# Layer 0 of a four-layer network: denominators of 256 queries per column strip, the turning matrix built first, keys on two queues, permuting copies further behind

## The chip, the cores and the metric

The kernel runs on one core of a Trainium2 chip. The metric is device microseconds of one execution of the whole program, all four layers. The core has five engines that run side by side, each in the order of its own instructions: TensorE (PE, with its weight loads as PEld), VectorE (DVE), ScalarE (ACT), GpSimd (POOL) and SyncE (SP), which here only issues DMAs. SyncE, ScalarE and GpSimd can each issue DMAs from a queue of their own; the 16 DMA engines behind the queues are shared.

## The reference

Only layer 0 is touched. It is attention over a 64x64 image with a learned bias for the relative row and the relative column, four heads of 32 channels, two images, all in f32:

```
x = x + conv_ref(group_norm(x))              # x: [2, 64, 64, 128]
q, k, v = split(group_norm(x) @ w_qkv)       # 4 heads of 32, L = 4096 positions
rw[q, m] = q . pos_emb_w[m],  rh[q, m] = q . pos_emb_h[m]   # m: relative column, row
scores = q k^T / sqrt(32) + shifted(rw) + shifted(rh)
out = softmax(scores) @ v
```

The two biases are products of q with the table of embeddings, shifted by one position per row so that a relative index becomes an absolute one (`rel_to_abs`).

## The kernel before

**Tiling.** Layer 0 goes through four units, a unit being one image b and one pair p of heads. A unit has eight query blocks (qb) of 512 queries, and each of these four key blocks (xb) of 1024 keys. For one key block the loop in `layer0` makes eight score tiles of 128 keys by 512 queries by two heads (matmuls at L806), whose exponentials ScalarE writes (L814); VectorE adds every tile into one accumulator `l0acc` (L817, L819), and 32 matmuls with v (L837) add to `l0o`. The accumulator, summed over its 128 partitions, is later the denominator.

**Bias by matmul.** The bias is not added: it is part of the score product. The keys' tile `ka` has, for each head, 32 rows of keys and 32 rows of one-hot patterns (made once on GpSimd by 16 instructions at L330), and the moving tile `l0mv` has 32 rows of q and 32 rows of bias: 16 for the row (`hd`, L681) and 16 for the column (`wd`, L676; for the very first block, four DMAs from `l0rw` in SBUF, L671). `fill` loads one `l0mv` per key block, two buffers in turn; for xb 2 and 3 it only loads `hd` anew. `prefill(at + 2)` at the end of each key block issues the load for two blocks later.

**Making the biases.** `biases` is a generator that yields 17 pieces for one unit. For the column bias, piece k (0 to 7): GpSimd turns q of one group g of 512 (`turned_q`, tile `l0tq`, L596), TensorE multiplies it with the turned embeddings (`l0pw`, L567), ScalarE or VectorE copies the result to SBUF (`l0ew`, L578 and L576), two DMAs store it to DRAM (`l0sw`, L581), two DMAs read it back with a skew (`l0tw`, L623), and GpSimd permutes that into `l0rw` (L605). The whole `l0rw` is stored as `wd` by four DMAs (L629). For the row bias (k from 8 on): `l0ph` (L567), `l0eh`, `l0sh`, and a skewed DRAM to DRAM copy to `hd` (L635).

**Prologue.** Before the loop the code goes once through the group norm of image 0 (`tokens`, norms at L474), `l0_constants` (a reversed identity called flip, made on GpSimd at L283 and L284, and matmuls at L296 that turn the embeddings with it), `project_k` (matmuls L509, copies L517 to `l0kst`, 16 DMAs to `ka`, L530), `project_q` (L541, copies to `l0xT`, four stores to `qd` in DRAM, L557), 11 of the 17 bias pieces of unit 0, and `project_v` (L488). The slope stores of even g go on ScalarE's queue here, all other DMAs on SyncE's. Then `prefill(0)` and `prefill(1)`.

**Side work.** What the later units need (the rest of the biases, the group norm and projections of image 1) is a list of generators per unit, `later`. `piece()` takes one yield of the list; the loop calls it once per key block, between scores and o matmuls, and once more after the o matmuls of xb 3.

**The end of a query block** is spread over the key blocks of the next one: `end_numerators` and `end_totals` at xb 0 (copy of `l0o`, L734; eight matmul instructions with a matrix of ones, `l0zb`, L741, that give the totals for all 512 queries on all four strips of 32 rows; a copy with a sum for a check, L749), `end_scale` at xb 1 (reciprocal on VectorE, 128x512, L752), `end_mult` at xb 2 (one multiply on GpSimd, L755), `end_fold` at xb 3 (matmuls L760 that add the two halves and turn the result, a second checked sum on ScalarE, L767, and the addition to x, L771). The strips 0 and 1 of `l0o` hold one half of the keys for heads 0 and 1, strips 2 and 3 the other half, so that a total is needed on both halves of the rows.

**What sets the order.** Layer 0 is under a manual schedule: each engine runs its instructions in the order in which the code writes them. So what stands ahead in the text on GpSimd's or SyncE's queue is waited for. The completion of DMAs on SyncE's and ScalarE's queues is counted on a set of semaphores shared by both, so an issue also waits until an earlier transfer that used the same semaphore has landed.

Of the kernel before, what the change touches and what calls it, by code (L numbers as in the profile page):

```python
# [8 lines left out]
F32 = mybir.dt.float32  # L9
# [29 lines left out]
class Net:  # L39
# [236 lines left out]
            )  # L276
        return raw

    def l0_constants(self, wp, ap, ps, raw):

        nc = self.nc
        flip = ap.tile([P, 512], F32, tag="os", name="l0flip")[:, :P]
        nc.gpsimd.memset(flip, 0.0)  # L283
        nc.gpsimd.affine_select(  # L284
            out=flip,
            in_=flip,
            compare_op=ALU.not_equal,
            fill=1.0,
            base=2 - 2 * S,
            pattern=[[1, P]],  # L290
            channel_multiplier=1,
        )
        pos = wp.tile([P, 2, P], F32, tag="pos", name="l0pos")
        for i in range(2):
            pt = ps.tile([P, 2, 512], F32, tag="pair", name=f"l0pe{i}")[:, 0, :]
            nc.tensor.matmul(  # L296
                pt[:, :P],
                lhsT=raw[:, i].rearrange("p h d -> p (h d)"),
                rhs=flip,
                start=True,  # L300
                stop=True,
            )
            nc.scalar.copy(pos[:, i, :], pt[:, :P])
        return pos
# [42 lines left out]
    def layer0(self):  # L347
# [7 lines left out]
        with ExitStack() as st:  # L355
# [18 lines left out]
            kd = dp.tile([2 * HD, L], F32, tag="kd", name="l0kd")  # L374

            mvs = [wp.tile([P, NX, 512], F32, tag=f"mv{i}", name=f"l0mv{i}") for i in range(2)]
            kas = self.l0_onehot(wp, ap, 2)

            def scratch(n):
# [38 lines left out]
            def tokens(ps, b):  # L418
# [40 lines left out]
                v = self.small.tile([P, 1], F32, tag="gv", name=f"gv{b}")  # L459
                nc.vector.scalar_tensor_tensor(v, d, d, mv[:, 1:2], ALU.mult, ALU.add)  # L460
                yield
                pv = bank(ps, f"gpv{b}")
                nc.tensor.matmul(pv[:, 0, 0:1], lhsT=self.gmat, rhs=v, start=True, stop=True)
                gr = self.small.tile([P, 1], F32, tag="gr", name=f"gr{b}")
# [39 lines left out]
            def project_k(ps, b):  # L504

                for x in range(NX):
                    pk = bank(ps, f"l0pk{b}_{x}")
                    for s in range(2):
                        nc.tensor.matmul(  # L509
                            pk[:, s, :].rearrange("p (a k) -> p a k", k=P),  # L510
                            lhsT=w[:, C : 2 * C],
                            rhs=halves(norm[b, x])[:, s],
                            start=True,
                            stop=True,
                        )
                    kst = staging(f"l0kst{b}_{x}").rearrange("p n q -> p (n q)")
                    nc.scalar.activation(  # L517
                        halves(kst),
                        pk.rearrange("p s (a k) -> p s a k", k=P),
                        AF.Copy,  # L520
                        scale=root,
                    )
                    cols = slice(x * TB * S, (x + 1) * TB * S)
                    for p in range(pairs):
                        if (b, p) == (1, 1):
                            nc.sync.dma_start(out=kd[:, cols], in_=kst[2 * HD :])
                            continue
                        for h in range(2):
                            at = (2 * p + h) * HD
                            nc.sync.dma_start(  # L530
                                out=kas[p][64 * h : 64 * h + HD, cols], in_=kst[at : at + HD]
                            )
                    yield

            def project_q(ps, b):

                xT = qTs[b]
                for x in range(NX):
# [18 lines left out]
                    nc.sync.dma_start(out=qd[b][:, cols], in_=xT[:, cols])  # L557
                    yield

            def slope(ps, u, n, g, tq):  # L560
# [25 lines left out]
            def biases(hold, u):  # L586
# [6 lines left out]
                def turned_q(g):  # L593
# [4 lines left out]
                        qTs[b].rearrange("p (x y) -> p y x", y=S)[:, 8 * g : 8 * g + 8, :],  # L598
                    )

                turned_q(0)
                for k in range(2 * 8 + 1):
                    if 2 <= k < 10:
                        g = k - 2
                        nc.gpsimd.tensor_copy(  # L605
                            rw.rearrange("p (x y) -> p y x", y=S)[:, 8 * g : 8 * g + 8, :],
                            tws.pop(g),
                        )
                    if k < 7:
                        turned_q(k + 1)  # L610
                    if 1 <= k < 9:
                        g = k - 1
                        if loop[0]:
                            tws[g] = ap.tile(
                                [P, 8, S], F32, tag="tw", name=f"l0tw{b}_{p}_{g}", bufs=1
                            )
                        elif g % 2 == 0:
                            tw2 = ap.tile(
                                [P, 2, 8, S], F32, tag="acc", name=f"l0tw{b}_{p}_{g}"
                            )  # L620
                            tws[g], tws[g + 1] = tw2[:, 0], tw2[:, 1]
                        for h in range(2):
                            nc.sync.dma_start(  # L623
                                out=tws[g][S * h : S * h + S],
                                in_=skewed(slopes[h, "w"][u], 8 * g, S, 8),
                            )
                    if k == 9:
                        for c in range(0, L, L // 4):
                            nc.sync.dma_start(  # L629
                                out=wd[u][:, c : c + L // 4], in_=rw[:, c : c + L // 4]  # L630
                            )
                    if k >= 9:
                        g = k - 9
                        for h in range(2):
# [22 lines left out]
            def fill(mv, u, qb, xb):  # L657
                b, p = u
                qs = slice(qb * 512, (qb + 1) * 512)
                for h in range(2):  # L660
                    at = (2 * p + h) * HD
                    if xb < 2:
                        near = u == units[0] and qb == 0
                        q = (qTs if near else qd)[b]
                        nc.sync.dma_start(
                            out=mv[64 * h : 64 * h + HD], in_=wide(q[at : at + HD, qs], HD)
                        )
                        if near:
                            for s in range(NX):
                                lo = 64 * h + TB * s  # L670
                                nc.sync.dma_start(  # L671
                                    out=mv[64 * h + 48 : 64 * h + 64, s],
                                    in_=rws[u][lo : lo + TB, qs],
                                )
                        else:
                            nc.sync.dma_start(  # L676
                                out=mv[64 * h + 48 : 64 * h + 64],
                                in_=wd[u][:, qs].rearrange("(h s r) q -> h r s q", h=2, r=TB)[h],
                            )
                    lo = S * h + S - TB * (xb + 1)  # L680
                    nc.sync.dma_start(  # L681
                        out=mv[64 * h + 32 : 64 * h + 48], in_=wide(hd[u][lo : lo + TB, qs], TB)
                    )

            first = [None]
            with tc.tile_pool(name="l0sp", bufs=4, space=PSUM) as ps:
                hold = [ps]
                for _ in tokens(ps, 0):
                    pass
                pos = self.l0_constants(wp, ap, ps, raw)  # L690
                for _ in project_k(ps, 0):
                    pass
                for _ in project_q(ps, 0):
                    pass
                first[0] = biases(hold, units[0])
                for _ in range(11):
                    next(first[0])
                for _ in project_v(ps, 0):
                    pass
# [34 lines left out]
                nc.scalar.copy(e.os, e.o)  # L734

            def end_totals(e):
                zb = ps.tile([P, 512], F32, tag="misc", name=f"l0zb{e.t}")
                for s in range(2):
                    for h in range(2):
                        at = 64 * s + HD * h  # L740
                        nc.tensor.matmul(  # L741
                            zb[at : at + HD, :],
                            lhsT=ones,
                            rhs=e.acc[:, h, :],
                            start=True,
                            stop=True,
                        )
                e.r = ap.tile([P, 512], F32, tag="zs", name=f"l0zs{e.t}", bufs=1)
                nc.scalar.activation(e.r, zb, AF.Copy, accum_out=sums[:, 0, e.n : e.n + 1])  # L749

            def end_scale(e):
                nc.vector.reciprocal(e.r, e.r)  # L752

            def end_mult(e):
                nc.gpsimd.tensor_tensor(e.os, e.os, e.r, ALU.mult)  # L755

            def end_fold(e):
                po = ps.tile([P, 4, 2 * HD], F32, tag="misc", name=f"l0po{e.t}")
                for i in range(4):
# [4 lines left out]
                        start=True,  # L764
                        stop=True,
                    )
                nc.scalar.activation(e.r, e.r, AF.Copy, accum_out=sums[:, 1, e.n : e.n + 1])  # L767
                b, p = e.u
                n0 = b * NC + 4 * e.qb
                xs = self.x[:, n0 : n0 + 4, p * 64 : p * 64 + 64]  # L770
# [8 lines left out]

            prefill(0)  # L780
            prefill(1)
            cur, prev = None, None
            for at, (i, qb, xb) in enumerate(order):
                u = units[i]
# [37 lines left out]
                if prev:  # L822
# [2 lines left out]
                    elif xb == 1:  # L825
                        end_scale(prev)
                    elif xb == 2:
                        end_mult(prev)
                    else:
                        end_fold(prev)  # L830
                piece()
# [12 lines left out]
                if xb == 3:  # L844
                    piece()
                prefill(at + 2)
            for part in (end_numerators, end_totals, end_scale, end_mult, end_fold):
                part(cur)
            while side:
                piece()  # L850
# [1289 lines left out]
```

## Time and profile before

| | us |
|---|---|
| four runs | 4851.39, 4856.27, 4859.64, 4865.56 |
| median | 4857.95 |
| profiled execution | 4860.4 |
| its span, first to last instruction | 4857.5 |
| layer 0, prologue (to the first full score block) | 0 to 120.8 |
| layer 0, loop and tail | 120.8 to 1671.9 |
| layers 1 to 3 | to 4857.5 |
| reciprocal L752, x32 | 3.34 to 3.35 each |
| multiply L755, x32 | 1.26 to 2.07 each |
| totals L741, eight instructions per block | 0.98 to 0.99 |

Over the span TensorE is busy 89%, VectorE 63%, ScalarE 49% and GpSimd 18%. These shares mix stages: in the prologue TensorE mostly waits (28.25 of 63 us between 54 and 117), and in the loop it is nearly always at work. So the prologue is read from the chain of waits and from the queue's own timeline, and the loop from windows between two reciprocals, one per query block. "SPq" is SyncE's issuing of a DMA, whose length is the time to issue; the landing stands apart, as "DMA".

### The profile page before, as it was taken

To read this page: it belongs to the slowest core of one execution; us is meant where nothing else is said; L and a number is where in the kernel's file an instruction comes from. 1 tells how busy PE (TensorE), PEld (TensorE's weight loads), DVE (VectorE), ACT (ScalarE), POOL (GpSimd) and SP (SyncE) were. 2 spreads that over 40 slices of the span, in tenths; PEclk is the share of its full clock that TensorE was granted. 3 is DMA by queue.
4 is the path that set the end of the run, shared out by engine and by line. 5 is a ranking of instruction groups with operands and counts; after the bars stand their busy time and mean duration, and the time that the engine had idled before them with its cause. 6 is when DMAs were issued, how large, how long until landed. Compare 5 with 4: busy or idle time off the path is not lost.

```text
span 4857.5 us, 67788 instructions
## 1 busy us (share of the span) xinstructions
PE 4326.8 (89%) x27079; PEld 1849.8 (38%) x27079; DVE 3048.0 (63%) x4776; ACT 2379.9 (49%) x2850; POOL 858.5 (18%) x561
## 2 busy tenths in 40 slices
PE   4999999999999755689999999949999999999765
PEld 2233333323333244322332333329974444444422
DVE  2898888989999888456666555550043333333577
ACT  1776677767766433257776888810022222222200
POOL 4110020210000121135554555500020000000000
PEclk6999999999999877789999999955589999999889
DMA  5452344453333100000000000023300000000000
GB/s 150 103 125 51 70 100 113 90 120 64 59 54 64 32 1 1 25 1 1 1 1 1 1 1 1 1 72 104 104 2 0 1 0 0 0 0 0 6 13 23
DMA packets 200790, 189.11 MB, mean 39 GB/s; under 512 B 83626, under 2 KB 137738, under 8 KB 200266
## 3 DMA queue, kind: packets, MB, share of 16 engines
q1 hardware_dynamic: 177546, 165.71, 15.5%
q10 hardware_dynamic: 22912, 18.89, 1.3%
q8 instruction: 218, 3.57, 0.3%
q14 instruction: 114, 0.93, 0.1%
HBM read 143.13 MB, written 45.09 MB: 39 GB/s over the span
## 4 chain that ended last, share of the span: by engine, by line
PE 68%; DVE 21%; ACT 4%; issue 3%; DMA 2%; POOL 1%; SPq 1%; DVEq 0%; ACTq 0%; POOLq 0%
PE l0sc L806 11%; DVE l0acc L819 10%; PE scl L1904 9%; PE oTl L1921 9%; PE l0o L837 5%; PE l2sc L1533 5%; PE l2pos L1434 4%; PE l2av L1585 4%; PE f3ex L2078 3%; PE f2po L1782 2%; PE f2ph L1756 2%; ACT l2es L1571 2%; DVE x L2086 1%; PE l2pu L1418 1%; DVE l2es L1557 1%
## 5 line engine op out<-in xcount | busy, mean ns | idle before, releaser
L819 DVE TENSOR_TENSOR l0acc<-l0acc,l0es 128x1024 f32<-128x1024 f32 x960 | 1226.0, 1277 | 125.5 <-ACT l0es L814 30.1
L814 ACT ACTIVATE l0es<-l0sc 128x1024 f32<-128x1024 f32 x1024 | 953.6, 1051 | 362.3 <-PE l0sc L806 342.0
L806 PE MATMUL l0sc<-l0mv,ka 64*64 64x512 f32 x8192 | 921.8, 597 | 18.5 <-issue 13.7
L1929 DVE TENSOR_TENSOR accl<-accl,esl 128x1024 f32<-128x1024 f32 x240 | 294.1, 1225 | 540.8 <-ACT esl L1915 482.8
L1560 POOL TENSOR_TENSOR l2es<-l2es 128x1024 f32<-128x1024 f32 (+3 forms) x288 | 505.6, 1756 | 603.8 <-DVE l2es L1557 533.3
L806 PEld LDWEIGHTS l0sc<-l0mv,ka 64*64 64x64 f32 x8192 | 295.0, 132 | 636.5 <-issue 296.6
L1571 ACT ACTIVATE l2es<-l2es 128x1024 f32<-128x1024 f32 (+3 forms) x576 | 533.3, 976 | 6.9 <-POOL l2es L1564 6.7
L1915 ACT ACTIVATE esl<-scl 128x1024 f32<-128x1024 f32 x240 | 245.8, 1024 | 550.4 <-PE scl L1904 550.4
L1557 DVE TENSOR_SCALAR l2es<-l2sc 128x1024 f32<-128x1024 f32 (+3 forms) x272 | 306.5, 1127 | 296.9 <-PE l2sc L1533 294.2
L1904 PE MATMUL scl<-l3qT,l3kT 128*128 128x512 f32 x1024 | 485.0, 596 | 1.8 <-DVE bok_l L254 1.8
L837 PE MATMUL l0o<-l0es,l0v 128*32 128x512 f32 x4096 | 465.6, 595 | 0.0
L1921 PE MATMUL oTl<-esl,l3v 128*128 128x512 f32 x960 | 448.5, 592 | 0.0
L1547 ACT ACTIVATE l2es<-l2sc 128x1024 f32<-128x1024 f32 (+3 forms) x288 | 273.7, 950 | 260.9 <-PE l2sc L1533 257.9
L1533 PE MATMUL l2sc<-l2q,l2kT 32*128 32x512 f32 (+3 forms) x2304 | 340.2, 624 | 10.1 <-DVE l2es L1557 5.9
L1585 PE MATMUL l2av<-l2es,l2v 128*32 128x512 f32 (+3 forms) x2304 | 321.6, 579 | 8.6 <-ACT l2es L1571 8.5
L1434 PE MATMUL l2pos<-l2v,toe 128*32 128x512 f32 (+3 forms) x2304 | 299.9, 581 | 1.4 <-ACT l2v L1379 1.4
L755 POOL TENSOR_TENSOR l0os<-l0os,l0zs 128x512 f32<-128x512 f32 x32 | 63.2, 1975 | 1300.3 <-DVE l0zs L752 1011.6
L1904 PEld LDWEIGHTS scl<-l3qT,l3kT 128*128 128x128 f32 x1024 | 193.1, 191 | 233.8 <-issue 219.2
L1921 PEld LDWEIGHTS oTl<-esl,l3v 128*128 128x128 f32 x960 | 182.4, 190 | 229.6 <-issue 225.8
L837 PEld LDWEIGHTS l0o<-l0es,l0v 128*32 128x32 f32 x4096 | 121.7, 109 | 311.3 <-issue 309.4
L1533 PEld LDWEIGHTS l2sc<-l2q,l2kT 32*128 32x128 f32 x2304 | 100.7, 189 | 255.3 <-ACT l2es L1571 91.5
L2086 DVE SCALAR_TENSOR_TENSOR x<-f3ex,f3wt,x 128x128 f32<-128x128 f32 x512 | 160.2, 347 | 28.5 <-PE f3ex L2078 20.0
(457 smaller groups left out, 4191.8 us busy)
## 6 DMA issues: line engine op xcount, KB each, us to landing
l0mv<-l0hd SPq DMA_DIRECT2D x256, 128.0 KB
l0mv<-l0qd SPq DMA_DIRECT2D x124, 256.0 KB
l0mv<-l0wd SPq DMA_DIRECT2D x124, 128.0 KB
l0sh<-l0eh SPq DMA_DIRECT2D x60, 144.0 KB
l0tw<-l0sw SPq DMA_DIRECT2D x64, 128.0 KB
l0wd<-l0rw SPq DMA_DIRECT2D x16, 512.0 KB
l0hd<-l0sh SPq DMA_DIRECT2D x64, 128.0 KB
f2w<-in_L_ffn_weight_dram ACTq DMA_DIRECT2D x32, 256.0 KB
```

The costliest lines, as they stand in the source:

```text
L806: nc.tensor.matmul(sc[64 * c : 64 * c + 64, h, :], lhsT=ka[rows, k0 : k0 + 64], rhs=mv[rows, NX - 1 - yb, :], start=True, stop=True,)
L814: nc.scalar.activation(es[yb, s], sc, AF.Exp)
L819: nc.vector.tensor_tensor(cur.acc, cur.acc, es[yb, s], ALU.add)
L837: nc.tensor.matmul(cur.o[lo : lo + HD, :], lhsT=v[:, 2 * (xb * NX + yb) + s, HD * h : HD * (h + 1)], rhs=es[yb, s][:, h, :], start=(xb == ...
L1434: nc.tensor.matmul(pos[c : c + 32, j0:, :], lhsT=toe[:, d * P + c : d * P + c + 32], rhs=v[:, n0 + j0 - d : n0 + 4 - d, :], start=(d == n0 ...
L1533: nc.tensor.matmul(sc[:, h2, off:], lhsT=kT[hs, cols], rhs=q[hs, off:], start=True, stop=True,)
L1557: nc.vector.tensor_scalar(es[:, :, lo:], sc[:, :, lo:], root, None, ALU.mult)
L1560: nc.gpsimd.tensor_tensor(part, part, part, ALU.mult)
L1571: nc.scalar.activation(e[:, :, off:], e[:, :, off:], AF.Silu)
L1585: nc.tensor.matmul(avs[i][hs, off:], lhsT=vs[b][:, k, hs], rhs=es[h // 2][:, h % 2, off:], start=(k == 0), stop=last,)
L1904: nc.tensor.matmul(sc[:, i, :], lhsT=kT[:, k * P : (k + 1) * P], rhs=qs, start=True, stop=True,)
L1921: nc.tensor.matmul(oT, lhsT=v[:, k, :], rhs=es[:, i, :], start=(k == 0), stop=(k == NC - 1),)
```

## The change

- `l0_flip` is split from `l0_constants` and called ahead of the one-hots.
- In the prologue the eight key DMAs of pair 1 are issued by GpSimd rather than SyncE.
- In the prologue the four stores of q to `qd` are taken out of `project_q` and written after `prefill(1)`.
- In the prologue the permuting copies of group g run in piece g + 4 rather than g + 2, and those left at k = 9; so GpSimd's order is tq 0 to 5, copy 0, tq 6, copy 1, tq 7, copies 2 to 7. 10 pieces run before the loop rather than 11.
- The first two fills read the column bias from `wd` in DRAM with one DMA per head rather than four from `l0rw`, 12 DMAs in all rather than 24, and the six of head 1 are issued by ScalarE.
- `tokens` yields once more between the two matmuls of the group statistics (L452 and L463).
- The totals are made for 256 queries per strip pair (half the columns), and so are the checked copy and the reciprocal. At xb 2 ScalarE copies each half across to the other rows (two copies of 64x256) and makes the second checked sum (before: at xb 3), and GpSimd multiplies in four instructions of 64x256.

```diff
@@ layer0
+            flip = self.l0_flip(ap)
             kas = self.l0_onehot(wp, ap, 2)
...
@@ tokens
                 yield
+                yield
                 pv = bank(ps, f"gpv{b}")
...
@@ project_k
-                            nc.sync.dma_start(
+                            queue = nc.gpsimd if p and not loop[0] else nc.sync
+                            queue.dma_start(
                                 out=kas[p][64 * h : 64 * h + HD, cols], in_=kst[at : at + HD]
...
@@ project_q
-                    nc.sync.dma_start(out=qd[b][:, cols], in_=xT[:, cols])
+                    if loop[0]:
+                        nc.sync.dma_start(out=qd[b][:, cols], in_=xT[:, cols])
...
@@ biases
+                    if loop[0] and 2 <= k < 10:
+                        permuted(k - 2)
                     if k < 7:
                         turned_q(k + 1)
+                    if not loop[0] and 4 <= k < 9:
+                        permuted(k - 4)
                     if 1 <= k < 9:
+                        shifted(k - 1)
                     if k == 9:
+                        for g in sorted(tws):
+                            permuted(g)
+                        stored()
...
@@ fill
+                    near = u == units[0] and qb == 0
+                    queue = nc.scalar if near and h and xb < 2 else nc.sync
...
-                        if near:
-                            for s in range(NX):
-                                lo = 64 * h + TB * s
-                                nc.sync.dma_start(
-                                    out=mv[64 * h + 48 : 64 * h + 64, s],
-                                    in_=rws[u][lo : lo + TB, qs],
-                                )
...
@@ prologue
-                for _ in range(11):
+                for _ in range(10):
                     next(first[0])
...
@@ end_totals
-                            rhs=e.acc[:, h, :],
+                            rhs=e.acc[:, h, 256 * s : 256 * s + 256],
...
@@ end_scale, end_cross in place of end_mult
+                nc.vector.reciprocal(e.r[:, 0, :], e.r[:, 0, :])
...
-                nc.gpsimd.tensor_tensor(e.os, e.os, e.r, ALU.mult)
+                for s in range(2):
+                    there, here = slice(64 - 64 * s, 128 - 64 * s), slice(64 * s, 64 * s + 64)
+                    nc.scalar.copy(e.r[there, 1, :], e.r[here, 0, :])
+                nc.scalar.activation(
+                    e.r[:, 0, :], e.r[:, 0, :], AF.Copy, accum_out=sums[:, 1, e.n : e.n + 1]
+                )
+                for s in range(2):
+                    rows = slice(64 * s, 64 * s + 64)
+                    for i in range(2):
+                        part = e.os[rows, 256 * i : 256 * i + 256]
+                        nc.gpsimd.tensor_tensor(part, part, e.r[rows, (s + i) % 2, :], ALU.mult)
...
@@ end_fold
-                nc.scalar.activation(e.r, e.r, AF.Copy, accum_out=sums[:, 1, e.n : e.n + 1])
...
@@ after the first fills
             prefill(0)
             prefill(1)
+            for x in range(NX):
+                cols = slice(2 * x * 512, 2 * (x + 1) * 512)
+                nc.sync.dma_start(out=qd[0][:, cols], in_=qTs[0][:, cols])
```

In `biases` the helpers `permuted`, `shifted` and `stored` hold the code that stood in the loop over k before (L605, L623 and L629).

More of the change, by code (lines that the diff above doesn't have):

```diff
@@ L277, in l0_raw, with l0_flip @@
         return raw
-    def l0_constants(self, wp, ap, ps, raw):
+    def l0_flip(self, ap):
         nc = self.nc
@@ L292, in l0_constants @@
         )
+        return flip
+    def l0_constants(self, wp, ps, raw, flip):
+        nc = self.nc
         pos = wp.tile([P, 2, P], F32, tag="pos", name="l0pos")
@@ L599, in turned_q, with permuted, shifted @@
                     )
+                def permuted(g):
+                    nc.gpsimd.tensor_copy(
+                        rw.rearrange("p (x y) -> p y x", y=S)[:, 8 * g : 8 * g + 8, :],
+                        tws.pop(g),
+                    )
+                def shifted(g):
+                    if loop[0]:
+                        tws[g] = ap.tile([P, 8, S], F32, tag="tw", name=f"l0tw{b}_{p}_{g}", bufs=1)
+                    elif g % 2 == 0:
+                        two = ap.tile([P, 2, 8, S], F32, tag="acc", name=f"l0tw{b}_{p}_{g}")
+                        tws[g], tws[g + 1] = two[:, 0], two[:, 1]
+                    for h in range(2):
+                        nc.sync.dma_start(
+                            out=tws[g][S * h : S * h + S],
+                            in_=skewed(slopes[h, "w"][u], 8 * g, S, 8),
+                        )
@@ L601, in biases, with stored @@
+                def stored():
+                    for c in range(0, L, L // 4):
+                        nc.sync.dma_start(
+                            out=wd[u][:, c : c + L // 4], in_=rw[:, c : c + L // 4]
+                        )
                 turned_q(0)
                 for k in range(2 * 8 + 1):
[L603 to L607, printed above, removed]
-                        )
+                    if loop[0] and 2 <= k < 10:
+                        permuted(k - 2)
@@ L609, in biases @@
                     if k < 7:
                         turned_q(k + 1)
+                    if not loop[0] and 4 <= k < 9:
+                        permuted(k - 4)
                     if 1 <= k < 9:
[L612 to L626, printed above, removed]
+                        shifted(k - 1)
                     if k == 9:
[L628 to L631, printed above, removed]
+                        for g in sorted(tws):
+                            permuted(g)
@@ L661, in fill @@
                     at = (2 * p + h) * HD
+                    near = u == units[0] and qb == 0
+                    queue = nc.scalar if near and h and xb < 2 else nc.sync
                     if xb < 2:
-                        near = u == units[0] and qb == 0
                         q = (qTs if near else qd)[b]
-                        nc.sync.dma_start(
+                        queue.dma_start(
                             out=mv[64 * h : 64 * h + HD], in_=wide(q[at : at + HD, qs], HD)
                         )
-                        if near:
-                            for s in range(NX):
-                                lo = 64 * h + TB * s
-                                nc.sync.dma_start(
-                                    out=mv[64 * h + 48 : 64 * h + 64, s],
-                                    in_=rws[u][lo : lo + TB, qs],
[L674 to L679, printed above, removed]
+                        queue.dma_start(
+                            out=mv[64 * h + 48 : 64 * h + 64],
+                            in_=wd[u][:, qs].rearrange("(h s r) q -> h r s q", h=2, r=TB)[h],
+                        )
                     lo = S * h + S - TB * (xb + 1)
-                    nc.sync.dma_start(
+                    queue.dma_start(
                         out=mv[64 * h + 32 : 64 * h + 48], in_=wide(hd[u][lo : lo + TB, qs], TB)
@@ L689, in layer0 @@
                     pass
-                pos = self.l0_constants(wp, ap, ps, raw)
+                pos = self.l0_constants(wp, ps, raw, flip)
                 for _ in project_k(ps, 0):
@@ L736, in end_totals @@
             def end_totals(e):
-                zb = ps.tile([P, 512], F32, tag="misc", name=f"l0zb{e.t}")
+                zb = ps.tile([P, 512], F32, tag="misc", name=f"l0zb{e.t}")[:, :256]
                 for s in range(2):
@@ L747, in end_totals, with end_cross @@
                         )
-                e.r = ap.tile([P, 512], F32, tag="zs", name=f"l0zs{e.t}", bufs=1)
-                nc.scalar.activation(e.r, zb, AF.Copy, accum_out=sums[:, 0, e.n : e.n + 1])
+                e.r = ap.tile([P, 2, 256], F32, tag="zs", name=f"l0zs{e.t}", bufs=1)
+                nc.scalar.activation(
+                    e.r[:, 0, :], zb, AF.Copy, accum_out=sums[:, 0, e.n : e.n + 1]
+                )
             def end_scale(e):
-                nc.vector.reciprocal(e.r, e.r)
-            def end_mult(e):
-                nc.gpsimd.tensor_tensor(e.os, e.os, e.r, ALU.mult)
+                nc.vector.reciprocal(e.r[:, 0, :], e.r[:, 0, :])
+            def end_cross(e):
+                for s in range(2):
+                    there, here = slice(64 - 64 * s, 128 - 64 * s), slice(64 * s, 64 * s + 64)
+                    nc.scalar.copy(e.r[there, 1, :], e.r[here, 0, :])
+                nc.scalar.activation(
+                    e.r[:, 0, :], e.r[:, 0, :], AF.Copy, accum_out=sums[:, 1, e.n : e.n + 1]
+                )
+                for s in range(2):
[3 more added lines that the diff above has]
+                        nc.gpsimd.tensor_tensor(part, part, e.r[rows, (s + i) % 2, :], ALU.mult)
             def end_fold(e):
@@ L827, in layer0 @@
                     elif xb == 2:
-                        end_mult(prev)
+                        end_cross(prev)
                     else:
@@ L846, in layer0 @@
                 prefill(at + 2)
-            for part in (end_numerators, end_totals, end_scale, end_mult, end_fold):
+            for part in (end_numerators, end_totals, end_scale, end_cross, end_fold):
                 part(cur)
```

## The prediction

> **What bounds it now.** Two parts of layer 0 are touched: the prologue up to 120.8 us and the loop to 1661.8; the rest (to 4857.5) is not. I read the chain of waits for the first 260 us first. Columns: start, length, what (us).
> ```profile
> 24.96 9.28 POOL ka L330 x4
> ...
> 34.30 0.20 POOL l0flip L283
> ...
> 34.57 0.29 POOL l0flip L284
> 34.87 18.26 issue
> ...
> 53.17 1.03 POOL l0tq L596
> ...
> 59.86 4.82 DMA l0sw<-l0ew
> ...
> 65.42 4.10 DMA l0tw<-l0sw
> ...
> 117.60 3.11 DMA l0mv<-l0hd
> 120.70 0.09 issue
> 120.79 9.16 PE l0sc L806 x58
> ```
> GpSimd's one-hots hold the turning matrix until 34.9, and TensorE's projections stand behind it; then a chain of small transfers runs to 120.8. Next, SyncE's timeline and its waits:
> ```profile
> 40.64 18.34 SPq L530 DMA_DIRECT2D ka<-l0kst  x16
> 59.41 4.11 SPq L557 DMA_DIRECT2D l0qd<-l0xT  x4
> 64.69 1.52 SPq L623 DMA_DIRECT2D l0tw<-l0sw  x2
> ...
> 99.75 2.77 SPq L629 DMA_DIRECT2D l0wd<-l0rw  x4
> ```
> ```profile
> SPq L530 <- DMA l0sw<-l0ew: 8.3, 1, 8.3
> ```
> The first slope load could issue at 64.69 only: keys, among them one hold of 8.3 for a transfer of the slopes, and the stores of q stood ahead of it. Last the loop by windows (columns: us, then busy time of PE, PEld, DVE, ACT, POOL, then PE clock, DMA share, GB/s):
> ```profile
> 1364.70:1409.95 45.25, 44.35 (x404) 14.30 (x400) 42.23 (x34) 31.62 (x38) 2.04 (x1) 1.00 0.34 59
> 194.69:245.84 51.15, 51.15 (x436) 15.21 (x432) 47.77 (x35) 37.35 (x44) 17.73 (x10) 1.00 0.48 109
> ```
> From one reciprocal to the next, 14 of the 31 periods take 45.25: 31 additions at a pitch of 1.33, a reciprocal of 3.35, and TensorE waits 0.9. VectorE bounds these. In the other 17 TensorE has side work and is full.
>
> **The prologue.** Turning matrix first: it costs 0.5 (0.20 + 0.29), the one-hots end at 34.7, hidden. Gone is TensorE's wait to 34.9; next late is the first norm (L474, ends 25.45; the others end by 32.45 and stay ahead of the k blocks, about 2.2 apart). So k and q move from 35.93 to 25.45, −10.5, and xT is whole at 42.6, not 53.1. But GpSimd now issues eight key DMAs behind its one-hots, before tq0. GpSimd issues none in this trace. Bounds from SyncE's rows: 0.59 each (the keys), 2.07 (L72, 8.29 for four). I take 1.02 (L72's first four, 4.06): 34.7 + 8.2 = 42.9, level with xT; at the upper end +8.4, at the lower nothing.
> The Trainium skill ("DMA: Bandwidth & Descriptors", Issuing engines are not separate DMA queues) says that a second issuing engine saves only the sequencer's time, usually small. The rule speaks against this part: by it the two queues save 8 x 0.59 = 4.7, while the row of 8.3 shows an in-order hold that it doesn't count.
>
> From tq0 at 42.9: tq 1.1, pw cold 2.0, copy 1.0, issue 0.4, sw landing 2.0 (74.92 in the chain; 4.82 when keys were landing): first tw at 49.1, where it was 64.69. The stores of q (4.11) are gone from ahead of it; they are now behind the first fills, hidden by the first two score blocks (price without cover: 4.1). Then SyncE repeats, per two slopes, four tw issues (0.65), two sw issues (0.5) and a wait for sw of about 2.1: 5.65, four times, 22.6. That the permuting copies run further behind takes them out of GpSimd's order ahead of tq: in the chain the copy at 69.66 held tq at 70.54, and 84.83 held 85.72. Last landing 3.0 and copy 1.05: wd stored from 75.7, not 99.75 (−24). From the store to the first full score block it was 21.0. Now: four stores 2.8, hd issue 2.5 and landing 3.5, then the chain's 3.11 for hd into mv with 0.3 ahead, 12.2: position rows come in one DMA for four, half of the fills go on ScalarE's queue (behind the v copies, before the table load), and one piece of the biases (wait 105.18 to 108.83) is no longer ahead. Loop start 75.7 + 12.2 = 87.9: **−32.9**. Bounds: +8.4 for sw landing at the contended 4.82 in some of the pairs instead of 2.0–2.7, or for GpSimd's queue; −4 if TensorE is warm (pw 1.1, not 2.0, four times). The piece left out (1.01) runs in the loop: **+1.0**.
>
> **The loop.** zb is eight matmul instructions, 0.98; at half the columns 0.49. In 17 TensorE-bound periods: 17 x −0.49 = **−8.3**; elsewhere nothing, TensorE waits there.
> The reciprocal is linear at best: 256 columns 1.70 by half of 3.35 plus a start, −1.65 in the 14 VectorE-bound periods. The multiply (2.04 beside additions, 1.26 alone) now stretches one addition from 1.23 to 2.11 (+0.88); that goes. Four multiplies of 64x256 come in. By GpSimd's 128x512 (1.26) and 128x1024 (L1095, 2.31), 256 columns are about 0.73. The old one costs VectorE 0.88 of its 1.26, so 0.38 less than it lasts; I take 0.73 − 0.38 = 0.35 each, +1.4. Together −1.65 − 0.88 + 1.4 = −1.1, 14 times: **−15.4**. Bounds: 0.88 each gives +14; nothing each gives −20 (TensorE's floor is 45.25 − 0.9 − 0.5).
> The Trainium skill ("SBUF — State Buffer", SBUF: two separate sides) says that GpSimd and a two-input VectorE instruction exclude each other for the whole instruction. By it a multiply costs 0.73 less the gap of 0.1, so 0.63, and the gain would be zero; the row shows 0.88 lost of 1.26, less than whole, and I keep 0.35.
>
> **New waits.** The multiplies stood behind the reciprocal only; now they wait for ScalarE's two crossing copies, which stand behind the eight exps of the same key block. Behind the multiplies on GpSimd are tq, rw. Mostly these are ready one piece ahead, but two tq are used at once, in the same block: unit 0, block 1, and unit 1, block 2. In the second, TensorE waits already:
> ```profile
> 656.85 1.08 PE L567 MATMUL l0pw<-l0tq,l0pos 32*72 32x512 f32 x4 [0.66 <-POOL l0tq L596]
> ```
> In the first the built order had tq ahead of the multiply (run at 99.6, far early); it now follows it. Counting from the end of the scores: last exp 1.3, crossing and sum 1.35 (0.59 for 128x512, 0.70 and 0.19), four multiplies beside the last additions 4.4, tq 2.0, gives 9.2 of wait, and 9.2 − 0.66 − 0.3 = 8.2 in the second. A long wait then costs clock too:
> ```profile
> 420.56 0.56 PE L463 MATMUL gpv<-gv,gmat 128*128 128x1 f32 x2 [6.73 <-DVE gv L460]
> 421.05 0.30 PEld L806 LDWEIGHTS l0sc<-l0mv,ka 64*64 64x64 f32 x8
> 421.05 9.22 PE L806 MATMUL l0sc<-l0mv,ka 64*64 64x512 f32 x64
> ```
> After 6.73 idle, scores took 9.22, not 7.03: 2.1 more. Sum 9.2 + 8.2 + 4.2 = **+21.6** (13 with everything at its uncontended time, 29 with multiplies at 2.04, 0 if other work covers it). Elsewhere rw is late behind the multiplies, then SyncE's tw loads and the fills behind them: some 4 places at 1–2, **+5** (0 to 10).
> The extra yield puts gpv one piece later, behind 3.6 of o matmuls; but gpm, whose own input comes from the same late VectorE (its statistics sit just ahead), then waits instead: **−0.7** (down to −8.8 if the wait goes whole). The tail (last period alone) has crossing copies 1.35 and four multiplies, less reciprocal 1.65 and the one multiply: **+0.3**.
>
> **Sum.** The profiled execution took 4860.4 (span 4857.5, 2.9 around it), 2.4 above the median. 4860.4 − 32.9 + 1.0 − 8.3 − 15.4 + 21.6 + 5 − 0.7 + 0.3 = **4831**; put against the median, 4829. I say 4830.
>
> **Rivals.**
> - *A, the forecast*, 4815 to 4843: 0.50. For it: the chain names the flip, and the order of SyncE's queue.
> - *B, the waits for tq don't bite* (exps end earlier than the scores' end suggests, or VectorE loses nothing): 4831 − 21.6 = 4809, with the full −20 in place of −15.4, 4805. For it: in before, such tq waits were 0.66. 0.20.
> - *C, the prologue keeps half its gain*: GpSimd's eight issues at 2.07 (+8.4) and contended landings (+8.4): 4848. Against it: DMA engines are 0.57 busy between 54 and 117, so they have room. 0.14.
> - *D, slower*: GpSimd's multiplies cost per instruction, not per column: 2.04 and 0.88 of VectorE each. VectorE-bound periods gain 4 x 0.88 − 2.53 = +1.0, 14 times, so +14 for −15.4; waits +7.5, late fills +5. 4831 + 29.4 + 12.5 = 4873. It decides from a loss of 0.63 each (2.53 / 4), where the loop's gain is nothing; only near 0.9 does it eat the prologue's too. Against it: 1.26 and 2.31 scale with columns. 0.13.
> - *The yield doesn't do what it says* is inside A (gpm waits for gpv's cause); if it does, −8.
> - 0.03 is left for something else, equally spread.
>
> About 0.2% (9.7 us) is what a measurement of this kernel can tell from no change: faster ends at 4848, slower begins at 4868. Faster: A 0.50, B 0.20, half of C 0.07 and 0.01: 0.78. Same: the other half of C and 0.01: 0.08. Slower: D and 0.01: 0.14. The range takes A, B and most of C: 4804 to 4854.
>
> **What would show it.** Right: k from 25.5; tq0 near 43; first tw near 49; stores of wd near 76; first full scores near 88; reciprocal 1.70 and multiplies 0.7–1.1; periods of 44.1 in units 2 and 3; waits of 8–9 ahead of l0pw, released by GpSimd, in unit 0 block 1 and unit 1 block 2. Wrong: GpSimd's key DMAs over 1.5 each; an addition that loses over 0.63 per multiply; no wait ahead of l0pw; gpv and gpm both without a wait.

## The result, and the profile after

The changed kernel takes 4865.47 us (median of 51 runs, 4847.82 to 4881.21), the kernel before 4861.25 (74 runs, 4845.51 to 4876.03) on the same chips. The ratio is 1.001, 95% interval 1.0004 to 1.0016: within 0.2%, where about 31 us less was forecast. The profiled execution has a span of 4871.6, 14.1 more than before. Of this, 11.4 lie in layers 1 to 3 (3197.1 against 3185.7), which the change doesn't touch; in the other profiles below they took 3177.6 to 3192.8. So parts are compared in layer 0, whose last addition to x ends at 1674.5 (before 1671.9). Each such time is that of one profiled execution. In the eight profiled kernels that share this prologue the scores began at 89.5 to 93.0, and one and the same loop, behind three different prologues, took 1523.0 to 1525.7; so a difference of some 3 us between two kernels tells little.

First the prologue. SyncE's timeline of the changed kernel (start, length, what):
```profile
30.89 7.49 SPq L538 DMA_DIRECT2D ka<-l0kst  x8
50.15 2.47 SPq L623 DMA_DIRECT2D l0tw<-l0sw  x2
...
77.30 3.99 SPq L630 DMA_DIRECT2D l0wd<-l0rw  x4
```
GpSimd's:
```profile
1.37 0.29 POOL L284 TENSOR_SCALAR_AFFINE_SELECT l0flip<-l0flip 128x128 f32<-128x128 f32 x1
...
2.58 32.17 POOL L335 TENSOR_TENSOR ka<-l0rev 32x1024 f32<-32x1024 f32 x16
34.70 4.07 POOL L538 DMA_DIRECT2D ka<-l0kst  x8
43.92 2.02 POOL L605 COPY l0tq<-l0xT 128x512 f32<-128x512 f32 x2 [5.15 <-DVE l0xT L561]
```
The matrix is ready at 1.7, the slopes are first read at 50.15 (before 64.69), and `wd` is stored from 77.30 (before 99.75). GpSimd waited 5.15 for xT behind its key DMAs, so these cost nothing. TensorE's scores begin at 92.21 and then run through (before: four of the first 64 instructions at 116.80, the rest from 120.79). The prologue gave 28.6.

Then the loop, which took all of it back. TensorE's timeline (xN: N instructions):
```profile
166.53 5.76 PE L829 MATMUL l0sc<-l0mv,ka 64*64 64x512 f32 x52
182.17 1.98 PE L576 MATMUL l0pw<-l0tq,l0pos 32*72 32x512 f32 x4 [9.88 <-POOL l0tq L605]
184.08 5.46 PE L860 MATMUL l0o<-l0es,l0v 128*32 128x512 f32 x32
...
238.74 7.10 PE L829 MATMUL l0sc<-l0mv,ka 64*64 64x512 f32 x64
...
247.69 1.08 PE L576 MATMUL l0pw<-l0tq,l0pos 32*72 32x512 f32 x4 [0.81 <-POOL l0tq L605]
248.70 3.64 PE L860 MATMUL l0o<-l0es,l0v 128*32 128x512 f32 x32
252.90 1.08 PE L576 MATMUL l0pw<-l0tq,l0pos 32*72 32x512 f32 x4 [0.56 <-POOL l0tq L605]
256.13 11.30 PE L829 MATMUL l0sc<-l0mv,ka 64*64 64x512 f32 x64 [2.15 <-DMA l0mv<-l0hd]
```
In the brackets stand the wait ahead and what ended it. Two kinds of loss are seen. At 182 TensorE waits 9.88 for l0tq (at 654 another 8.90). At 247 to 256 it waits three times, 3.5 in all, the last time because the fill of l0mv is late, and the 64 score instructions then take 11.30, not 7.10 as at 238.74. GpSimd's timeline has the reason for both:
```profile
175.30 5.71 POOL L776 TENSOR_TENSOR l0os<-l0os,l0zs 64x256 f32<-64x256 f32 x4 [98.03 <-ACT l0zs L769]
181.07 2.04 POOL L605 COPY l0tq<-l0xT 128x512 f32<-128x512 f32 x2
...
237.20 6.56 POOL L776 TENSOR_TENSOR l0os<-l0os,l0zs 64x256 f32<-64x256 f32 x4 [18.83 <-ACT l0zs L769]
243.82 2.00 POOL L611 COPY l0rw<-l0tw 128x512 f32<-128x512 f32 x1
245.63 2.00 POOL L605 COPY l0tq<-l0xT 128x512 f32<-128x512 f32 x1
```
Here four multiplies last 5.7 and 6.6 (4.7 to 6.8 over the loop, median 6.0), where one lasted 2.06. They begin when ScalarE is done, and l0tq and l0rw come behind them. SyncE's waits in the stretch from 228.68 to 285.45 show how this reaches the fills; below, the same query block of the kernel before (line, what it waited for: us in all, times, longest).
```profile
SPq L623 <- POOL l0rw L611: 19.3, 2, 18.7
```
```profile
SPq L623 <- POOL l0rw L605: 10.5, 2, 9.4
```
The tw load waits for its buffer, which l0rw's copy frees, and the fills stand behind that load in SyncE's queue, as its timeline in the changed kernel shows:
```profile
245.84 1.26 SPq L623 DMA_DIRECT2D l0tw<-l0sw  x2
...
248.19 0.39 SPq L682 DMA_DIRECT2D l0mv<-l0qd  x1
...
250.50 0.42 SPq L690 DMA_DIRECT2D l0mv<-l0hd  x1
```
By windows from one reciprocal to the next (columns as in the prediction), a quiet period and this one in the changed kernel, and last this one before (the quiet one before, 1364.70 to 1409.95, stands in the prediction):
```profile
1374.49:1418.98 44.49, 44.29 (x408) 14.56 (x408) 41.12 (x35) 32.38 (x40) 5.92 (x4) 1.00 0.34 60
228.68:285.45 56.77, 53.25 (x420) 17.41 (x416) 43.91 (x35) 36.48 (x44) 17.22 (x11) 0.94 0.51 132
```
```profile
245.84:294.04 48.20, 48.20 (x412) 14.29 (x408) 44.91 (x35) 34.56 (x41) 11.15 (x6) 1.00 0.60 156
```
The quiet period fell from 45.25 to 44.1–44.5; VectorE is busy 41.1 of it, not 42.2. The other rose from 48.20 to 56.77, and TensorE's clock fell to 0.94. Three more periods are like it: they were 49.70, 51.37, 52.48 and are 56.22, 56.92, 59.86. These four, "the late blocks", lost 28.0 together; they are the later query blocks in which GpSimd makes the column bias of the next unit. In them TensorE waits 14.9 more in all (18.3, before 3.3), and the other 13.1 are time in which it is busy, for the most part at a lower clock.

### The profile page after: what moved, and what is told of

The parts are those of the page before. It is cut to its first block, busy times and chain, and to the rows that moved or that the text cites. A ratio compares the mean times of both kernels' runs of the same rounds, so it can differ in the third digit from the quotient of the medians.

```text
span 4871.6 us, 67920 instructions
## 1 busy us (share of the span) xinstructions
PE 4342.5 (89%) x27079; PEld 1873.6 (38%) x27079; DVE 3001.9 (62%) x4776; ACT 2394.6 (49%) x2914; POOL 972.0 (20%) x665
## 4 chain that ended last, share of the span: by engine, by line
PE 49%; DVE 10%; ACT 4%; issue 2%; DMA 1%; POOL 0%; SPq 0%; ACTq 0%; DVEq 0%; POOLq 0%
PE scl L1927 9%; PE oTl L1944 9%; PE l2sc L1556 5%; PE l2pos L1457 4%; PE l2av L1608 4%; PE f3ex L2101 3%; PE f2po L1805 2%; PE f2ph L1779 2%; ACT l2es L1594 2%; DVE x L2109 1%; DVE l2es L1580 1%; PE l2pu L1441 1%; DVE l1t L1146 1%; ACT l2es L1570 1%; PE l2po L1515 1%
## 5 line engine op out<-in xcount | busy, mean ns | idle before, releaser
L829 PE MATMUL l0sc<-l0mv,ka 64*64 64x512 f32 x8192 | 933.8, 602 | 31.9 <-DMA l0mv<-l0hd 29.9
L829 PEld LDWEIGHTS l0sc<-l0mv,ka 64*64 64x64 f32 x8192 | 305.1, 133 | 652.1 <-issue 314.1
L776 POOL TENSOR_TENSOR l0os<-l0os,l0zs 64x256 f32<-64x256 f32 x128 | 186.5, 1476 | 1207.6 <-issue 821.7
L1927 PEld LDWEIGHTS scl<-l3qT,l3kT 128*128 128x128 f32 x1024 | 193.1, 191 | 233.7 <-issue 219.1
```

What stands on the lines that cost most here:

```text
L829: nc.tensor.matmul(sc[64 * c : 64 * c + 64, h, :], lhsT=ka[rows, k0 : k0 + 64], rhs=mv[rows, NX - 1 - yb, :], start=True, stop=True,)
L1927: nc.tensor.matmul(sc[:, i, :], lhsT=kT[:, k * P : (k + 1) * P], rhs=qs, start=True, stop=True,)
```

## The experiments

Theory 1: the loss comes from GpSimd's order. The new multiplies, behind ScalarE and ahead of l0rw and l0tq, cause both kinds. Rival 1: the pieces, moved by one slot, cause the late blocks. In the edits, minus is the base and plus the experiment. A table at the end of this section gives layer 0's own times.

**Prologue alone.** The changed kernel with before's denominators.
```diff
-                            rhs=e.acc[:, h, 256 * s : 256 * s + 256],
+                            rhs=e.acc[:, h, :],
...
-                        end_cross(prev)
+                        end_mult(prev)
```


> The changed kernel with the denominators of before (totals, reciprocal and one multiply of 512 columns). Theory 1 (the new multiplies, placed behind ScalarE and ahead of the copies of the biases on GpSimd, cost the loop about 48 us: 20 in two waits for l0tq and 28 in four query blocks where l0rw, the tw loads and the fills come late): loop start near 92, none of these waits, about 28 us less than before, 4831 to 4835. Rival 1 (it is the side pieces, which begin one slot later, that make the copies late): the four query blocks stay at 56 to 60 us, and the time is 4850 to 4860.

Median 4845.47, ratio 0.9969 (0.9957 to 0.998); layer 0 ends 21.5 earlier than before. The late blocks are back at 49.62, 49.60, 51.30 and 51.74: rival 1 falls. The gain in layer 0 is 7 short of 28 (the median is 15 under before's 4860.82 in the same set of runs), mostly because the extra yield costs here (three periods +4.3 together; TensorE waits 6.60 for gpm and 3.23 later), and the first l0pw waits 2.54 even behind one multiply.

**Denominators alone.** Before, with the new `end_totals`, `end_scale`, `end_cross` and `end_fold`.


> The kernel before with only the new denominators. Theory 1: prologue as before (120.8), one wait of about 9 for l0tq (unit 1, block 2; in unit 0 the first l0tq is still issued ahead), four query blocks some 7 longer each, quiet ones 1 shorter: 10 + 28 - 17 = about +20, 4880. Rival 1: without the shifted pieces only the one wait is left, 10 - 17 = -7, 4854.

Median 4873.71, ratio 1.0035 (1.0021 to 1.005); layer 0 ends 14.4 later. One wait of 8.90, late blocks of 54.89, 57.00, 56.18 and 59.71 (+26.0), quiet periods of 44.12. Theory 1 holds: the denominators bring the late blocks with them.

**Multiplies behind the piece.** Only the place of the four multiplies in the program is changed.
```diff
                         end_cross(prev)
...
                 piece()
+                if prev and xb == 2:
+                    end_mult(prev)
                 v = vs[u]
```


> The changed kernel with the four multiplies written behind the side piece of the same key block, so behind l0rw and l0tq on GpSimd. Theory 1: both waits of 9 to 10 and most of the 28 go, the quiet blocks stay at 44.3: 45 us less than the changed kernel, about 4820. Rival 1: only the two waits go, 4846. Against both: l0po may wait for the multiplies at key block 3, at most 1 to 2 us in eight or so blocks.

Median 4812.91, ratio 0.9907 (0.989 to 0.9923); layer 0 ends 56.5 earlier than in the changed kernel. The expected 45 is exceeded, since the late blocks fall 8.7 below before's too; so the order may have cost something in the kernel before as well, with its one multiply, but that was not tested. The same stretch as 228.68 to 285.45 above:
```profile
218.17:266.27 48.10, 48.10 (x416) 14.31 (x409) 44.14 (x35) 35.29 (x44) 14.90 (x9) 1.00 0.58 147
```
TensorE is busy throughout at the full clock. Both waits for l0tq are gone, the late blocks are 48.10, 47.57, 49.84 and 47.61, and l0po waits for no multiply in the loop. This shows the cause: the same multiplies, just as long (median 6.0 for four), hold up nobody behind the copies. What they cost VectorE stays: the quiet periods are 44.1 to 44.5 as in the changed kernel.

**One multiply in the old place.** ScalarE makes four crossing copies into a tile of 128x512.
```diff
-                    nc.scalar.copy(e.r[there, 1, :], e.r[here, 0, :])
+                    nc.scalar.copy(full[there, s, :], e.r[here, 0, :])
+                    nc.scalar.copy(full[here, s, :], e.r[here, 0, :])
...
+                nc.gpsimd.tensor_tensor(
+                    e.os, e.os, full.rearrange("p i q -> p (i q)"), ALU.mult
+                )
```


> The changed kernel with four crossing copies on ScalarE into one tile and one multiply of 128x512 on GpSimd, in the old place. If the length of the four multiplies (6 us) is what holds the copies: the waits for l0tq shrink to 5 or 6 each and the four late blocks by some 5 each, 28 us less than the changed kernel, about 4838. If the wait for ScalarE is what holds them (theory 1, second form): the two waits stay at 9 and the time within 8 us of the changed kernel, 4858 to 4866.

Median 4834.71, ratio 0.9949 (0.9935 to 0.9963); layer 0 ends 29.1 earlier than in the changed kernel. The late blocks fall by 17.6 of their 28 (51.00, 54.46, 50.76, 55.94), so mostly the length of the four makes them. But the waits for l0tq stay at 7.56 and 7.47, and my 5 to 6 was too low. Of the 7.56, 3.3 pass until ScalarE is done, 2.2 in the multiply and 2.0 in the first copy of l0tq, which took 1.0 in the changed kernel.

**Tw loads on GpSimd's queue**, in the changed kernel.
```diff
-                        nc.sync.dma_start(
+                        queue = nc.gpsimd if loop[0] else nc.sync
+                        queue.dma_start(
                             out=tws[g][S * h : S * h + S],
```


> The changed kernel, but in the loop GpSimd issues the tw loads, so that SyncE's fills no longer stand behind a load that waits for l0rw. If the late fills are what makes four query blocks 5.5 to 8.6 longer: these come back to within 2 of before (48 to 52 us), no score block waits for hd there, and the time is some 22 under the changed kernel, 4843. If the waits for l0tq and the cold TensorE make them: they stay at 54 or more. Against it: GpSimd then waits for the slopes to land ahead of l0rw and l0tq, and each issue costs it about 0.5 (four per piece), which can make l0tq later still; the two waits of 9 to 10 stay in any case.

Median 4850.14, ratio 0.9982 (0.9972 to 0.9993); layer 0 ends 17.0 earlier. The late blocks are 52.14, 53.73, 51.78 and 56.63. Neither outcome was met whole: of 28, 15.5 went with the late fills, and 12.5 stay. No score waits for hd in the first three, but l0tq is later there (waits of 0.93 and 1.89 in the first, where it was 0.81 and 0.56), now also behind GpSimd's own issues (1.4 for two). In the fourth hd is late still (4.97), and 4.1 of the 12.5 lie there. So the late fills are at least half of that loss; how the rest is shared between them and l0tq stays open, since the experiment itself makes l0tq later.

The next four stand on the kernel with the multiplies behind the piece.

**One multiply behind the piece**: the edits of both.


> The changed kernel with four crossing copies, one multiply of 128x512, and that multiply behind the side piece. If order on GpSimd and the additions that the multiplies stretch are the two costs, they add: quiet query blocks at 43.85 rather than 44.3 (12 of them, -5.5), the rest as with four multiplies behind the piece: about 4807. If ScalarE's two more copies cost as much as they save, it stays at 4813.

Median 4802.05, ratio 0.9871 (0.9849 to 0.9892); layer 0 ends 5.5 earlier, quiet periods 43.6 to 44.2. The two costs add, as expected.

**The yield ahead of gpm.**
```diff
                 nc.vector.bn_aggr(mv, st)
                 yield
+                yield
...
-                yield
                 yield
                 pv = bank(ps, f"gpv{b}")
```


> Four multiplies behind the piece, and the added yield moved from between gpm and gpv to ahead of gpm. If TensorE waits only because the statistics are late in VectorE's queue by one piece: the wait of 5.8 ahead of gpm and the cold scores after it (2) go, 4805. If VectorE is simply behind by so much, the same time is waited for somewhere later (at l0zb or at gpv): 4811 to 4814.

Median 4805.18, ratio 0.9873 (0.9853 to 0.9893); layer 0 ends 7.0 earlier. The wait of 5.76 ahead of gpm is gone and its period is 48.19, not 54.70; two waits of 1.79 and 1.43 are left. So a piece more between VectorE's statistics and gpm was wanted, not between gpm and gpv.

**Keys on one queue.**
```diff
-                            queue = nc.gpsimd if p and not loop[0] else nc.sync
+                            queue = nc.sync
```


> Four multiplies behind the piece, all sixteen key DMAs of the prologue on SyncE. If the second queue is what freed the slopes: the hold of 8 us is back, first tw near 58, loop start 8 later, 4821. If the earlier start alone freed them (16 issues from 30.9 at 0.59 end at 40.5, ahead of the first tw at 50): no difference, 4813.

Median 4810.52, ratio 0.9885 (0.9865 to 0.9904): no difference to be measured. SyncE issues all sixteen from 30.89 to 41.0, the first tw is at 50.12, and the scores start at 94.96, 2.0 later than in the base and 2 to 5.4 later than in the eight kernels with this prologue and two queues. So the second queue is worth some 2 to 5 us; the hold of 8 is not back, since the keys are now issued well ahead of the slopes.

**Flip late.**
```diff
-            flip = self.l0_flip(ap)
             kas = self.l0_onehot(wp, ap, 2)
+            flip = self.l0_flip(ap)
```


> Four multiplies behind the piece, the turning matrix built behind the one-hots as before. If the matrix held TensorE's queue as the chain shows: the k blocks start at 36, everything up to the loop 10 later, 4823. If another thing had been late next (norms, GpSimd's key DMAs): 3 to 5 later only, 4817.

TensorE's timeline:
```profile
35.02 1.23 PE L301 MATMUL l0pe<-l0flip,l0raw 128*128 128x128 f32 x4 [15.02 <-POOL l0flip L284]
36.04 9.50 PE L516 MATMUL l0pk<-l0mv,wqkv 128*128 128x512 f32 x16
```
The k blocks start at 36.04 and the scores at 102.65, 9.7 later: the matrix alone holds about a third of the prologue's gain. Layer 0 ends 7.6 later. The median, 4819.40, has the ratio 0.9906 (0.9886 to 0.9927); across two sets of runs it can't be told from 0.9907, so only the trace shows this. What the stores of q, the copies further behind and the shorter first fills each gave of the rest was not tested apart.

**All three**: one multiply, behind the piece, and the yield ahead of gpm.


> The changed kernel with one multiply of 128x512, that multiply behind the side piece, and the added yield ahead of gpm. If the three edits touch different blocks, they add: layer 0 ends 5.5 earlier than with the one multiply behind the piece and 7 earlier for the yield, at about 1605.5, and the time is 66 to 68 under before, ratio 0.986. If they share VectorE's slack, the yield brings 2 or less: 1610.

Median 4791.52, ratio 0.9858 (0.9838 to 0.9879); layer 0 ends at 1604.4. The edits add. This is the fastest version, 1.4% under before. Its quiet periods, 43.86 each, are now bound by TensorE, which never waits in this stretch of two of them:
```profile
1200.00:1287.00 87.00, 87.00 (x796) 28.29 (x792) 80.55 (x67) 64.93 (x82) 4.54 (x2) 1.00 0.35 61
```

| kernel | scores begin | layer 0 ends | the four late blocks, sum |
|---|---|---|---|
| before | 116.8 (in full 120.8) | 1671.9 | 201.8 |
| changed | 92.2 | 1674.5 | 229.8 |
| prologue alone | 91.1 | 1650.4 | 202.3 |
| denominators alone | 116.1 (120.0) | 1686.3 | 227.8 |
| multiplies behind the piece | 93.0 | 1618.1 | 193.1 |
| one multiply, old place | 89.5 | 1645.4 | 212.2 |
| tw loads on GpSimd | 93.0 | 1657.5 | 214.3 |
| one multiply behind the piece | 91.2 | 1612.5 | 195.5 |
| yield ahead of gpm | 92.3 | 1611.0 | 194.8 |
| keys on one queue | 95.0 | 1620.7 | 195.2 |
| flip late | 102.7 | 1625.7 | 190.8 |
| all three | 91.4 | 1604.4 | 193.5 |

## Why the prediction was wrong

The time lies 11.5 above the range. Term by term in layer 0, from the profile:

| step | forecast | measured |
|---|---|---|
| prologue | −32.9 | −28.6 |
| piece moved into the loop | +1.0 | +1.1 |
| zb in TensorE-bound periods | −8.3 | −3.4 |
| quiet, VectorE-bound periods | −15.4 | −11.5 |
| two waits for l0tq, with the clock | +21.6 | +20.5 |
| **l0rw, tw loads and fills late** | **+5** | **+28.0** |
| gpm in place of gpv | −0.7 | −2.1 |
| the last period and the tail | +0.3 | −1.5 |
| sum | −29.4 | +2.5 |

The rows don't cut alike: the forecast for zb is for 17 periods, the measured −3.4 for the eight that stand in no other row. There it is 0.42 each, not 0.49: by the timeline the eight instructions take 0.64, where they took 1.07 before (0.99 in the chain's rows), so half the columns did not bring half the time.

- **The step that failed** is "Elsewhere rw is late behind the multiplies, then SyncE's tw loads and the fills behind them: some 4 places at 1–2, +5 (0 to 10)". The mechanism and the number of places are right; the size is not: 5.6 to 8.6 each. Two things were left out. The late pieces come in a row, so in three of the four blocks TensorE waits for l0tq twice and then for the fill; and short waits cost clock too, as the same prediction has it for a long one (in the first late block 3.5 of waiting and 4.5 of slow scores). The upper bound of 10 was a guess per place, not worked out from a row, and that made the range too narrow.
- **The multiplies** were right alone (0.71, forecast 0.73) and so was VectorE's loss (an addition goes from 1.23 to 1.57, 0.34 each, forecast 0.35). Beside additions I took 1.1; it is 1.62 (median of 128). So four last 6.0 (median), where 4.4 was reckoned.
- **Rival D** had the sign of this term, with another price: not VectorE's 0.88 each but GpSimd's own time. The trace had the row that gives it: the old multiply took 2.04 beside additions and 1.26 alone, a wait of 0.8; four instructions wait four times. That its 4873 lies near the measured 4865 is luck: its +14 for the quiet periods came out as −11.5.
- **The prologue** missed 4.3: 1.6 by the time `wd` is stored, and 2.7 from there to the scores, in waits of the stores and fills for earlier fills' transfers (2.1 ahead of a store, 1.6 and 1.1 ahead of the position rows). Key DMAs on GpSimd took 0.51 each, under the bounds I gave. The sum up to the first tw also slips: 42.9 and its five steps make 49.4, not 49.1 (measured 50.15).
- **The lock on the shared port** (the Trainium skill, "SBUF — State Buffer", SBUF: two separate sides) would have made the quiet periods' gain zero, by the prediction's estimate of 0.63 for each multiply. An addition lost 0.34, and the 14 periods gained 0.82 each. There the trace was the better guide.
- **The two waits for l0tq** were forecast within 1, and the cause, the order of the instructions on GpSimd, is right. That the size fits is partly luck: the four multiplies took 5.7 in the first, not 4.4, and the copy of l0tq 1.0, not 2.0 (and the terms of the 9.2 add up to 9.05). The waits were in the sum, but no alarm to me: two waits of 9 meant that the multiplies are in the wrong place, and the same was true of the blocks beside them.

## What to carry to other kernels

Splitting one instruction into four on an engine that shares its time with another multiplies the waits, not only the work: price each piece beside its neighbour, as the trace shows it, and then ask what is queued behind it. Work that is needed late (here a product wanted one key block later) belongs behind copies that others wait for; moving the four multiplies behind them was worth 56 us of layer 0. And when one step of a chain is late, follow it through every in-order queue to the end before giving it a bound.

## What the runs showed of the hardware

- GpSimd's 64x256 multiply: 0.71 alone, 1.62 beside VectorE's additions, so that four take turns with four additions and last 6.0 (median).
- TensorE slowed down after waits much shorter than the 6.73 in the prediction. In the late block at 718 to 729 none was longer than 1.26 (0.53, 0.56, 1.08, 1.26 within 11 us), and the scores took 10.84 without the wait; this window shows the clock at 0.72:
```profile
726.00:738.40 12.40, 10.79 (x66) 3.80 (x67) 5.40 (x6) 7.06 (x9) 2.75 (x2) 0.72 0.71 154
```
  The Trainium skill ("TensorE: Matmul & The Clock Gate", HAM oscillation — how this bites in real kernels) gives the rule that TensorE should have no idle gap over some 3.4 us. None of these four was that long. Nor does their sum decide it. With the tw loads on GpSimd, 1.04 and 1.89 left the clock at 1.00 over the next 9 us, 0.65 and 1.88 in the same order brought 0.81 (last column but two):
```profile
957.60:966.60 9.00, 8.99 (x78) 2.39 (x80) 6.89 (x6) 7.86 (x10) 5.66 (x6) 1.00 0.66 159
719.80:728.80 9.00, 9.00 (x64) 2.98 (x68) 4.43 (x5) 6.87 (x8) 3.66 (x5) 0.81 0.68 160
```
  And with the yield ahead of gpm, waits of only 0.43 and 1.04 (at 981 to 983.7) were followed by 9 us at 0.81, while the single wait of 2.54 in the prologue-alone kernel left it at 1.00. What exactly is counted stays open.
